# Sorted rows transposed by the DMA queue, and two more buffers for neighbour rows, in a graph kernel with quantile aggregation

## The chip, the cores and the metric

The kernel runs on one core of a Trainium2 chip. A core has five engines that run side by side, each with its own in-order queue of instructions: TensorE (PE; PEld is its loading of weights), VectorE (DVE), ScalarE (ACT), GpSimd (POOL) and SyncE (SP, which here only issues transfers). They meet at semaphores. SBUF holds the working tiles, PSUM what TensorE writes, DRAM the rest. The metric is the device time of one execution in microseconds (us), the median of several runs; less is better.

## The reference

16 graphs of 1024 nodes with 64 channels go through two layers. What is computed:

```python
# layer 0, for each node: drop some neighbours by rank, then quantiles over the rest
nb = (adj_ > 0) & ~eye;  m = nb.sum(-1);  rank = cumsum(nb) - 1
skip = where(m > 10, (m + 1) // 2, 1)
removed = nb & (skip > 1) & mask & ((rank + 1) % skip == 0)
adj_d = where(removed | removed.T, 0, adj_)
agg = 0.25 * q25 + 0.5 * q50 + 0.25 * q75     # of x over the neighbours left, per channel, interpolated
y = relu((x + agg) @ W1 + b1) @ W2 + b2
x = layernorm(x + y * mask)
# layer 1
dh = tanh(concat(x, adj @ x) @ W1' + b1') @ W2' + b2'
x = layernorm(x + dh)
```

The edge update of layer 1 does not reach the output. About 1.6% of the node pairs are edges, so a node has some 10 to 30 neighbours after the dropping. The quantiles need each node's neighbours sorted, channel by channel.

## The kernel before

The graphs are handled in groups of 2, 4, 4, 4 and 2 (`GROUPS`). A group passes through three stages, and stages of different groups run side by side: while one group is in its quantiles, the lists of the next are made and the messages of the one before are finished.

**Lists** (`list_batch`, one graph after the other, in 8 tiles of 128 nodes). SP loads a tile of adjacency `a` (L622, a pool of three buffers that the messages use too) and the tile's rows of `x` into the tail of a row buffer `nb` (L625). DVE makes `nb`, the 0/1 row in bf16 (L623, L626). ACT counts it, TensorE ranks it (L652 to L660), ACT and DVE find the removed neighbours, TensorE and ACT write the kept ones back into `nb` (L672 to L677). Then the nodes of the graph are sorted by their number of neighbours (L685 to L708), and POOL writes each `nb` tile, row by row, to its sorted place in DRAM, in `order` (L712, an indirect DMA, a scatter). An `nb` buffer can be filled anew only after its scatter has read it. `nb` has NT + 1 = 9 buffers for 8 tiles per graph, so tile t of the next graph takes the buffer of tile t-1. `gone`, the removed ones, has 8.

**Quantiles.** After sorting, nodes with like numbers of neighbours lie together, and a group is cut into chunks (`CHUNKS`) that share one number of slots k. For each chunk `fill` puts the neighbours' `x` into slots `slots_a`, and `select` runs a network of min and max on DVE over them (L875), weighs the quantiles on ACT and PE (L897, L899), computes the layer, and scatters the result `y` to DRAM (L916). There are two kinds of fill:

- `Chunk`: DVE extracts the neighbours' numbers from the rows (L825, L827) and POOL gathers `x` by them, one indirect DMA for each slot and tile (L846, 1012 in all).
- `ChunkByPE` (the fourth entry of a `CHUNKS` tuple is 1): TensorE selects rows. For each pair of graphs, which is called a pass here (32 in all), SP loads two blocks of 128 sorted rows x 1024 from `order` into `row_p` (L957, two buffers). TensorE transposes each in 8 blocks of 128 x 128 into PSUM (L960, the single buffer with tag "tr", which the transposes of `nb` at L652 use too), and ACT copies it into `val` (L961), whose two halves are those of the two graphs. TensorE adds up ranks over the nodes and ACT writes them back into `val` (L966 to L970). For each slot k DVE makes a 0/1 matrix `hot` by `val == k` (L982), and TensorE multiplies it with `x`, which was split into three bf16 parts (L990). ACT copies the result into the slots (L1001). `val` has one buffer, so ACT's copy for the next pass waits for the last `hot` of this one; `row_p` waits only for TensorE.

**Messages** (`messages`): layer 1, one graph after the other. `a` is loaded again (L1024), transposed by TensorE (L1029), multiplied with `x` (L1039); DVE adds up `d` (L1049).

The source weaves the stages with `Side.advance`: in each chunk 24 shares are given out, and each stage advances by its part. The order of instructions on an engine is then set by a planner when the program is built, which works from the source's order and from when it expects buffers and inputs to be ready. SP is one in-order queue for all loads but the indirect ones: `a`, `x`, `row`, `row_p`, `degs`, `srt` and slot 0. POOL's queue holds the gathers and both kinds of scatter.

A slow general path behind the fast one (`tc.If(general > 0)`, from L1155 on) is not run with these inputs.

Of the kernel before, what the change touches and what calls it, by code (L numbers as in the profile page):

```python
# [9 lines left out]
F32 = mybir.dt.float32  # L10
F16 = mybir.dt.float16
BF16 = mybir.dt.bfloat16
# [3 lines left out]
ALU = mybir.AluOpType  # L16
# [4 lines left out]
P = 128  # L21
# [6 lines left out]
BINS = 64  # L28
# [388 lines left out]
def kernel(  # L417
# [15 lines left out]
    nc = tc.nc  # L433
    B, N, C = x.shape
    H = w1a.shape[1]
    NT = N // P
# [11 lines left out]
    const = ctx.enter_context(tc.tile_pool(name="const", bufs=1))  # L448


    ident = const.tile([P, P], F32, name="ident")
    make_identity(nc, ident)
    ident_h = const.tile([P, P], BF16, name="ident_h")
    nc.vector.tensor_copy(ident_h, ident)
    off_diag = const.tile([P, P], BF16, name="off_diag")
    nc.vector.tensor_scalar(off_diag, ident, -1.0, 1.0, op0=ALU.mult, op1=ALU.add)
    upper = const.tile([P, P], F32, name="upper")
    nc.gpsimd.memset(upper, 1.0)
    nc.gpsimd.affine_select(out=upper, in_=upper, compare_op=ALU.is_ge, fill=0.0, base=0,
                            pattern=[[1, P]], channel_multiplier=-1)  # L460
    off_diag_f = const.tile([P, P], F32, name="off_diag_f")
    nc.vector.tensor_copy(off_diag_f, off_diag)
    minus_h = const.tile([P, P], BF16, name="minus_h")
    nc.vector.tensor_scalar(minus_h, ident, -1.0, None, op0=ALU.mult)
    far_h = const.tile([P, P], BF16, name="far_h")
# [6 lines left out]
    ones_h = const.tile([P, P], BF16, name="ones_h")  # L472
# [9 lines left out]
    nc.vector.memset(big[:, 1:2], -BIG)  # L482
    eps = const.tile([P, 1], F32, name="eps")
    nc.vector.memset(eps, EPS)
    zero = const.tile([P, BINS], F32, name="zero")
    nc.vector.memset(zero, 0.0)
    number = const.tile([P, B * NT], F32, name="number")
    nc.gpsimd.iota(number, pattern=[[P, B * NT]], base=0, channel_multiplier=1,
                   allow_small_or_imprecise_dtypes=True)
# [92 lines left out]

    sort = ExitStack()
    rows = sort.enter_context(tc.tile_pool(name="rows", bufs=2))
    held = sort.enter_context(tc.tile_pool(name="held", bufs=NT + 1))
    work = sort.enter_context(tc.tile_pool(name="work", bufs=2))
    nets = sort.enter_context(tc.tile_pool(name="nets", bufs=2))
    hbm = sort.enter_context(tc.tile_pool(name="hbm", bufs=1, space=DRAM))
    ps_t = sort.enter_context(tc.tile_pool(name="ps_t", bufs=1, space=PSUM))
# [22 lines left out]
    def list_batch(g, b):  # L612

        nbs, gone = [], []
        for half_b in range(2):
# [3 lines left out]
            for t in range(half_b * HT, (half_b + 1) * HT):  # L619
# [8 lines left out]
                for h in range(2):  # L628
# [15 lines left out]
                                           op0=ALU.is_gt, op1=ALU.mult)  # L644
# [3 lines left out]
            for t in range(half_b * HT, (half_b + 1) * HT):  # L648
                nb, r, col = nbs[t], gone[t], slice(t - half_b * HT, t - half_b * HT + 1)
                p = ps_t.tile([P, N], BF16, name="p_nb", tag="tr")  # L650
# [5 lines left out]
                for h in range(2):  # L656
                    p = ps_m.tile([P, HALF], F32, name="p_rank", tag="rv", bufs=3)
# [9 lines left out]
        for t in range(NT):  # L667
            blk = slice(t * P, (t + 1) * P)
            for h in range(2):
                cols = slice(h * HALF, (h + 1) * HALF)  # L670
                p = ps_m.tile([P, HALF], F32, name="p_val", tag="rv", bufs=3)
# [19 lines left out]
        p = ps_m.tile([P, 512], F32, name="p_tot", tag="m")  # L691
        for t in range(NT):
            nc.tensor.matmul(p[:, :BINS], ones_h, own[:, t], start=t == 0, stop=t == NT - 1)
        base = work.tile([P, BINS + 1], F32, name="base", bufs=1)
        nc.vector.memset(base[:, 0:1], 0.0)
        nc.vector.tensor_tensor_scan(base[:, 1:], zero, p[:, :BINS], 0.0, op0=ALU.add, op1=ALU.add)
        p = ps_m.tile([P, NT, BINS], F32, name="p_at", tag="m")
        nc.tensor.matmul(p, ident, base[:, None, :BINS].to_broadcast([P, NT, BINS]), start=True, stop=False)
        for t in range(NT - 1):
# [222 lines left out]
    class ChunkByPE(Chunk):  # L922
# [13 lines left out]
        def fill(self):  # L936
            g, low = self.g, self.net["low"]
# [4 lines left out]
            at0 = self.t0 * g.run  # L942
            slots = self.net["slots"]
            inside = {at: k for k, at in enumerate(slots)}
            for q in range(g.count // 2):
# [7 lines left out]
                    nc.vector.tensor_scalar(free[:, k - low], degs[:, :, :, 0], float(k), None, op0=ALU.is_le)  # L953
                val = nets.tile([P, NT, 2, P], BF16, name="val", bufs=1)
                for i in range(2):
                    row = nets.tile([P, N], BF16, name="row_p")
                    nc.sync.dma_start(row, g.order[2 * q + i][at0:at0 + P, :N // 2].bitcast(BF16))  # L957
                    p = ps_t.tile([P, NT, P], BF16, name="p_row", tag="tr")
                    for j in range(NT):
                        nc.tensor.transpose(p[:, j], row[:, j * P:(j + 1) * P], ident_h)  # L960
                    nc.scalar.copy(val[:, :, i], p)  # L961

                for c in range(NT - 2, -1, -2):
                    p = ps_m.tile([P, 2, 2 * P], F32, name="p_nth", tag="rv", bufs=3)
# [8 lines left out]
                for s0 in range(0, self.k, 4):  # L973
                    p = ps_m.tile([P, 4, P], F32, name="p_slots", tag="rv", bufs=3)
                    for s in range(s0, min(s0 + 4, self.k), 2):
# [5 lines left out]
                        for e, at in enumerate(duo):  # L981
                            nc.vector.tensor_scalar(hot[:, :, :, e], val, float(inside[at]), None,  # L982
                                                    op0=ALU.is_equal)
# [72 lines left out]
    def prepare(g):  # L1056
        for b in range(g.b0, g.b0 + g.count):
            yield from list_batch(g, b)
        yield from weigh_group(g)
# [37 lines left out]
    for s in range(-LEAD, len(plan)):  # L1097
        j = s + LEAD
# [17 lines left out]
        if s >= 0:  # L1116
            i = plan[s][0]
# [40 lines left out]
    rows = ctx.enter_context(tc.tile_pool(name="rows_g", bufs=2))  # L1158
    held = ctx.enter_context(tc.tile_pool(name="held_g", bufs=NT))
    work = ctx.enter_context(tc.tile_pool(name="work_g", bufs=1))  # L1160
    ones_row = work.tile([P, N], BF16, name="ones_row")
    nc.vector.memset(ones_row, 1.0)  # L1162
    ps_t = ctx.enter_context(tc.tile_pool(name="ps_t_g", bufs=2, space=PSUM))
# [94 lines left out]
    with tc.tile_pool(name="dense", bufs=1) as dense, tc.If(general > 0), tc.For_i(0, B, 1) as b:  # L1258
# [5 lines left out]
        val = dense.tile([P, NT, N], BF16, name="val")  # L1264
        val_t = dense.tile([P, NT, N], BF16, name="val_t")
        for t in range(NT):
            v = neighbours(t, kept, removed, deg[:, t:t + 1])
            nc.vector.tensor_copy(val[:, t], v)
            p = ps_t.tile([P, NT, P], BF16, name="p_val", tag="tr")
# [7 lines left out]
        with tc.For_i(0, C, 1) as c:  # L1277
# [3 lines left out]
            for h in range(2):  # L1281
                p = ps_t.tile([P, HT, P], F32, name="p_row", tag="ta")
# [5 lines left out]
            for k in range(NT):  # L1288
# [3 lines left out]
                if k + 1 < NT:  # L1292
                    nc.vector.tensor_scalar(before[:, k, k + 1:], x_r[:, k + 1:], x_k, None, op0=ALU.is_ge)
                nc.vector.scalar_tensor_tensor(before[:, k, k], x_r[:, k], x_k, upper,
                                               op0=ALU.is_equal, op1=ALU.mult)
                nc.vector.scalar_tensor_tensor(before[:, k, k], x_r[:, k], x_k, before[:, k, k],
                                               op0=ALU.is_gt, op1=ALU.add)
            part = dense.tile([P, NT, 2], F32, name="part")
            for t in range(NT):
                for h in range(2):  # L1300
                    cols = slice(h * HALF, (h + 1) * HALF)
                    js = slice(h * HT, (h + 1) * HT)
                    p = ps_m.tile([P, 512], F32, name="p_cnt", tag="m")
# [5 lines left out]
                    for i, (_, share) in enumerate(TAUS):  # L1309
# [5 lines left out]
                        else:  # L1315
# [3 lines left out]
                                                   op0=ALU.mult, op1=ALU.mult,  # L1319
# [31 lines left out]
```

## Time and profile before

| | us |
|---|---|
| median of 4 runs (3128.2 to 3146.86) | 3137.62 |
| the profiled execution | 3127.18 |
| its span, first to last instruction | 3125.5 |
| PE / DVE / ACT / POOL busy | 2370.9 / 2391.6 / 1575.6 / 1695.1 |
| POOL gathers L846, 1012 of 1336 ns | 1352.3 |
| DVE min and max L875, three largest groups | 356.2, 285.7, 197.5 |
| PE L990 (12288 matmuls) | 694.9 |
| scatter of `nb`, L712, 128 of 1133 ns | 145.0 |
| mean granted TensorE clock | 0.889 of full speed |

In the lines of the profile, "PE p_row L960" is the instruction of line 960 on PE that writes the tile p_row; an arrow `out<-in` names what it writes and reads. In a list of groups, "x512 | 45.3, 226 | 15.9 <-ACT val L961 13.3" is: 512 instructions, busy for 45.3 us together, 226 ns the mean of one; before them the engine stood idle for 15.9 us, of which 13.3 ended when ACT's instruction of L961 was done. In a list of waits, "A <- B: 73.6, 29, 20.4" is: A waited for B, 73.6 us in total, in 29 waits, the longest 20.4. In the slices, the span is cut into 40 equal parts of 78 us, and each digit is the busy share in tenths. In a timeline each row has its start, its length and, in brackets, the engine's idle time before it and what ended it. "SPq" is SP's queue, which issues transfers; what it waits for is the condition of the transfer.

### The profile page before, as it was taken

The page shows a single profiled execution, that of the slowest core. Times are in us where ns is not written, and L with a number is a line of the kernel's source. Part 1 is how long each engine was busy: PE and PEld are TensorE (multiplying, and loading weights), DVE is VectorE, ACT ScalarE, POOL GpSimd, SP SyncE. Part 2 cuts the span into 40 slices and gives each one's busy share as a digit, 9 for nine tenths or more (in the row PEclk, how much of TensorE's full clock was granted, in tenths as well). Part 3 has the DMA queues.
Part 4 walks back from the last instruction along what each step waited for, and adds up shares of the span by engine and source line. Part 5 has one row for each costly group of instructions (what it writes and reads, how often), then busy time and mean ns, then how long its engine had stood idle before and what let it go on. Part 6 is the DMA issues. An engine that isn't in the chain of part 4 may idle for free. (4 is left out here: it accounts for less than half of the span.)

```text
span 3125.5 us, 65767 instructions
## 1 busy us (share of the span) xinstructions
PE 2370.9 (76%) x24920; PEld 1885.5 (60%) x25076; DVE 2391.6 (77%) x5580; ACT 1575.6 (50%) x4045; POOL 1695.1 (54%) x1512
## 2 busy tenths in 40 slices
PE   4456875769686997859888997787799376677977
PEld 2244663457574776647767775576677365466755
DVE  3359984679799889969999888888999397666741
ACT  5624656746354556544566566334464244243543
POOL 3165774356587376766663866485456555343300
PEclk9778998889898998989999998898899698888988
DMA  2520433333323333243334243123232231122222
GB/s 94 163 58 21 117 111 99 103 89 100 90 67 84 103 100 83 47 121 106 89 94 125 64 129 96 40 62 118 69 82 65 64 84 43 54 73 53 80 64 79
DMA packets 221333, 264.34 MB, mean 85 GB/s; under 512 B 147443, under 2 KB 148050, under 8 KB 221008
## 3 DMA queue, kind: packets, MB, share of 16 engines
q1 hardware_dynamic: 174288, 189.31, 20.8%
q0 software_dynamic: 46720, 70.74, 8.7%
q8 instruction: 199, 3.26, 0.4%
q14 instruction: 126, 1.03, 0.1%
HBM read 218.20 MB, written 46.40 MB: 85 GB/s over the span
## 5 line engine op out<-in xcount | busy, mean ns | idle before, releaser
L846 POOL DMA_INDIRECT slots_a<-in_x_dram,idx x1012 | 1352.3, 1336 | 724.7 <-issue 265.5
L990 PE MATMUL p_slots<-hot,parts 128*64 128x256 bf16 (+1 forms) x12288 | 694.9, 269 | 135.2 <-DVE hot L982 130.2
L990 PEld LDWEIGHTS <-parts 128*64 128x64 bf16 x12288 | 631.6, 113 | 174.0 <-issue 99.1
L875 DVE TENSOR_TENSOR slots_b<-slots_a 128x256 f32<-128x256 f32 (+14 forms) x582 | 356.2, 627 | 96.8 <-DMA slots_a<-in_x_dram,idx 64.7
L916 POOL DMA_INDIRECT x<-y,ids x128 | 174.0, 1359 | 361.0 <-DVE y L558 214.7
L982 DVE TENSOR_SCALAR hot<-val 128x2048 bf16<-128x2048 bf16 x456 | 308.4, 694 | 20.1 <-PE p_slots L990 16.6
L899 PE MATMUL p_g<-ident,terms 128*64 128x128 f32 x1988 | 279.2, 293 | 57.5 <-ACT terms L897 56.9
L899 PEld LDWEIGHTS p_g<-ident,terms 128*64 128x64 f32 x1988 | 238.3, 148 | 90.4 <-ACT terms L897 72.6
L875 DVE TENSOR_TENSOR slots_a<-slots_b 128x256 f32<-128x256 f32 (+11 forms) x526 | 285.7, 555 | 0.6
L1039 PE MATMUL p_msg<-adj_t,x_n 128*64 128x128 f32 x2048 | 277.2, 289 | 7.9 <-ACT adj_t L1030 4.2
L1039 PEld LDWEIGHTS p_msg<-adj_t,x_n 128*64 128x64 f32 x2048 | 237.3, 145 | 31.8 <-issue 10.6
L630 ACT ACTIVATE gone<-nb 128x512 bf16<-128x512 bf16 x256 | 159.9, 628 | 157.6 <-DVE nb L626 156.0
L1001 ACT COPY slots_a<-p_slots 128x512 f32<-128x512 f32 (+2 forms) x136 | 73.0, 537 | 300.2 <-PE p_slots L990 246.1
L1029 PE MATMUL p_adj<-ident,a 128*128 128x128 f32 x1024 | 185.8, 295 | 43.5 <-ACT adj_t L1030 22.1
L660 PE MATMUL p_rank<-reach,nb_t 128*128 128x128 bf16 (+3 forms) x956 | 172.7, 312 | 58.9 <-ACT nb_t L654 50.7
L662 ACT ACTIVATE gone<-p_rank,s 128x512 bf16<-128x512 f32 x256 | 166.2, 684 | 97.1 <-PE p_rank L660 82.1
L825 DVE MAX8 key<-code 128x8 f16<-128x1024 f16 x170 | 207.2, 1219 | 1.7
L875 DVE TENSOR_TENSOR slots_b<-slots_b 128x256 f32<-128x256 f32 (+11 forms) x310 | 197.5, 637 | 0.4
L712 POOL DMA_INDIRECT order<-nb,at_i x128 | 145.0, 1133 | 94.8 <-issue 40.6
L660 PEld LDWEIGHTS <-nb_t 128*128 128x128 bf16 x1024 | 95.2, 103 | 164.5 <-ACT nb_t L654 78.1
L1049 DVE TENSOR_TENSOR d<-p_d,b2b_r 128x64 f32<-128x64 f32 x128 | 28.1, 219 | 209.3 <-PE p_d L1048 206.7
L1030 ACT COPY adj_t<-p_adj 128x512 f32<-128x512 f32 x256 | 149.4, 583 | 75.4 <-PE p_adj L1029 73.3
(189 smaller groups left out, 4573.7 us busy)
## 6 DMA issues: line engine op xcount, KB each, us to landing
a<-in_adj_dram SPq DMA_DIRECT2D x256, 512.0 KB
row_p<-order SPq DMA_DIRECT2D x64, 256.0 KB
slots_a<-in_x_dram,idx POOLq DMA_INDIRECT x1012
row<-order SPq DMA_DIRECT2D x192, 64.0 KB
nb<-in_x_dram SPq DMA_DIRECT2D x128, 32.0 KB
row<-order SPq DMA_DIRECT2D x32, 128.0 KB
x_s<-in_x_dram SPq DMA_DIRECT2D x16, 256.0 KB
x_n<-x SPq DMA_DIRECT2D x16, 256.0 KB
```

Of the source, the lines that this page charges most:

```text
L630: nc.scalar.activation(r[:, cols], nb[:, cols], AF.Copy, accum_out=m[:, h, t - half_b * HT:t - half_b * HT + 1])
L660: nc.tensor.matmul(p[:, c * P:], nb_t[:, (h * HT + c) * P:(h * HT + c + 1) * P], reach[:, :HALF - c * P], start=False, stop=c == HT - 1)
L662: nc.scalar.activation(r[:, h * HALF:(h + 1) * HALF], p, AF.Abs, bias=biases[h][:, col], scale=2.0)
L825: nc.vector.max(key[:, t, r:r + 8], code)
L846: nc.gpsimd.indirect_dma_start(out=self.a[:, at[k], t, :], out_offset=None, in_=x_rows, in_offset=bass.IndirectOffsetOnAxis(ap=idx[:, t, k ...
L875: nc.vector.tensor_tensor(view(rb, ra, [(d[0], d[1 + side]) for d in dims]), view(ab, aa, [(d[0], d[1]) for d in dims]), view(bb, ba, [(d[ ...
L899: nc.tensor.matmul(p[:C, col], terms[:, i], ident, start=False, stop=t == e - 1 and first + i == places - 1)
L916: nc.gpsimd.indirect_dma_start(out=g.x1, out_offset=bass.IndirectOffsetOnAxis(ap=g.local[:, self.t0 + t:self.t0 + t + 1], axis=0), in_=y[: ...
L982: nc.vector.tensor_scalar(hot[:, :, :, e], val, float(inside[at]), None, op0=ALU.is_equal)
L990: nc.tensor.matmul(p[i * C:(i + 1) * C, o:o + w], g.parts[2 * q + i][:, c, h], hot[:, c, i, :w], start=c == 0 and h == 0, stop=c == NT - 1 ...
L1029: nc.tensor.transpose(p[:, j, :], a[:, col:col + P], ident)
L1039: nc.tensor.matmul(p[C:2 * C, :QUART], x1[:, j, :], adj_t[:, j, :], start=(j == 0), stop=(j == NT - 1))
```

## The change

Three edits:

1. The two blocks of sorted rows of a pass in `ChunkByPE.fill` are transposed by the transfer itself: a DMA transpose, issued on SP, reads 128 rows x 1024 bf16 from `order` and writes 128 partitions x 8 x 128 straight into one half of `val`. The tile `row_p`, TensorE's 16 transposes and ACT's two copies of a pass are gone.
2. `held`, the pool of the `nb` tiles, has NT + 3 = 11 buffers and no longer 9.
3. Two constants leave the memory of the fast path. `off_diag` in bf16 is made only for the general path, and `off_diag_f` comes straight from `ident`. `zero` is gone: the running sum in `list_batch` multiplies by ones where it added zeros. With `row_p` (4096 bytes in each partition), `zero` and `off_diag` (256 each) they make up most of the 4640 bytes that two more `nb` tiles take.

```diff
-    off_diag = const.tile([P, P], BF16, name="off_diag")
-    nc.vector.tensor_scalar(off_diag, ident, -1.0, 1.0, op0=ALU.mult, op1=ALU.add)
...
-    nc.vector.tensor_copy(off_diag_f, off_diag)
+    nc.vector.tensor_scalar(off_diag_f, ident, -1.0, 1.0, op0=ALU.mult, op1=ALU.add)
...
-    zero = const.tile([P, BINS], F32, name="zero")
-    nc.vector.memset(zero, 0.0)
...
-    held = sort.enter_context(tc.tile_pool(name="held", bufs=NT + 1))
+    held = sort.enter_context(tc.tile_pool(name="held", bufs=NT + 3))
...
-        nc.vector.tensor_tensor_scan(base[:, 1:], zero, p[:, :BINS], 0.0, op0=ALU.add, op1=ALU.add)
+        nc.vector.tensor_tensor_scan(base[:, 1:], ones_h[:, :BINS], p[:, :BINS], 0.0, op0=ALU.mult, op1=ALU.add)
...
                 val = nets.tile([P, NT, 2, P], BF16, name="val", bufs=1)
                 for i in range(2):
-                    row = nets.tile([P, N], BF16, name="row_p")
-                    nc.sync.dma_start(row, g.order[2 * q + i][at0:at0 + P, :N // 2].bitcast(BF16))
-                    p = ps_t.tile([P, NT, P], BF16, name="p_row", tag="tr")
-                    for j in range(NT):
-                        nc.tensor.transpose(p[:, j], row[:, j * P:(j + 1) * P], ident_h)
-                    nc.scalar.copy(val[:, :, i], p)
+                    nc.sync.dma_start_transpose(
+                        val[:, :, i], g.order[2 * q + i][at0:at0 + P, :N // 2].bitcast(BF16))
...
+    off_diag = work.tile([P, P], BF16, name="off_diag")
+    nc.vector.tensor_copy(off_diag, off_diag_f)
     ones_row = work.tile([P, N], BF16, name="ones_row")
```

## The prediction

> **What bounds the kernel now.** I read the page's shares and slices first, then the list of waits, then the waits of SP's queue, then the timeline where a long wait lies, and last the tiles that the change touches.
>
> ```profile
> PE 2370.9 (76%) x24920; PEld 1885.5 (60%) x25076; DVE 2391.6 (77%) x5580; ACT 1575.6 (50%) x4045; POOL 1695.1 (54%) x1512
> ...
> PE   4456875769686997859888997787799376677977
> ...
> DVE  3359984679799889969999888888999397666741
> ```
>
> No engine is the bound by itself. DVE is nearly full from slice 9 to slice 31, PE close behind, and the idle time (734 us on DVE) lies at the start, at the end and in lumps between. So a saving counts where it closes a lump, and only in part where it makes one of two full engines shorter.
>
> ```profile
> DVE nb L626 <- DMA order<-nb,at_i: 73.6, 29, 20.4
> ...
> SPq L625 <- DMA order<-nb,at_i: 369.0, 80, 67.0
> ...
> SPq L957 <- PE p_row L960: 209.6, 29, 53.7
> ```
>
> The first two lines are the buffers: DVE stood 73.6 us in 29 waits, and SP's queue 369 us, until a scatter had read an old `nb`. The last is the queue waiting for a `row_p` buffer. The largest lump, by the timeline from 803 to 830 us:
>
> ```profile
> 819.73 1.00 POOL L846 DMA_INDIRECT slots_a<-in_x_dram,idx  x1 [0.30 <-DMA slots_a<-in_x_dram,idx]
> 821.03 1.00 POOL L846 DMA_INDIRECT slots_a<-in_x_dram,idx  x1 [0.30 <-issue]
> 823.67 0.98 POOL L712 DMA_INDIRECT order<-nb,at_i  x1 [0.17 <-issue]
> 824.96 0.96 POOL L712 DMA_INDIRECT order<-nb,at_i  x1 [0.30 <-issue]
> 826.22 1.12 POOL L712 DMA_INDIRECT order<-nb,at_i  x1 [0.30 <-issue]
> 826.53 0.69 DVE L626 TENSOR_SCALAR nb<-a 128x1024 bf16<-128x1024 f32 x1 [20.45 <-DMA order<-nb,at_i]
> 827.26 0.63 ACT L630 ACTIVATE gone<-nb 128x512 bf16<-128x512 bf16 x1 [21.89 <-DVE nb L626]
> ```
>
> The scatter stands behind a row of gathers of 1.3 us each on POOL; DVE waits 20.45 us for the first one, about 2.9 us after its issue, and ACT behind it. The transposes that the change removes:
>
> ```profile
> L960 PE MATMUL p_row<-ident_h,row_p 128*128 128x128 bf16 x512 | 45.3, 226 | 15.9 <-ACT val L961 13.3 <-DMA row_p<-order 2.1 <-ACT nb_t L654 0.4
> L961 ACT COPY val<-p_row 128x1024 bf16<-128x1024 bf16 x64 | 64.7, 1012 | 28.3 <-DVE hot L982 11.3 <-PE p_row L960 10.4 <-DVE low L687 6.3
> ```
>
> Pipelined, 512 transposes are 45.3 us of busy PE, not 512 x 226 ns; ACT's copies are 64.7 us. Their loads come early: SP issued them up to 196 us before the first copy that uses them.
>
> **What the Trainium skill says.** "DMA: Bandwidth & Descriptors", section on the anatomy of one DMA: a DMA has about 2.0 us of fixed time, and a wait for a semaphore happens on the issuing sequencer, before dispatch. The trace agrees: the SP queue stands still in L625 and L957 while nothing behind them leaves. The same page, "Rules for kernel authors", has the DMA transpose issued from SP or ACT only, so the change can't leave that in-order queue for GpSimd's; no run here shows a transpose yet. The two prices below are from that page (latency section: 261 GB/s with a non-contiguous middle dimension) and from "VectorE: DVE Perf Modes", the three transpose paths (1309 ns for 128x128 bf16 by DMA, 390 ns by TensorE; the trace has 219 ns as TensorE's median, so the page's figures are not this kernel's).
>
> **The change, part by part.** The profiled execution is 3127.2 us, 3125.5 of it span; its time is 10 us under the median of 3137.6. I make the sum on its trace and move the median by it.
>
> *Buffers of `nb`, 9 to 11.* Tile t of the next batch takes the buffer of tile t-3 and no longer of t-1, so tiles 1 and 2 also run ahead of the scatter, and tile 3 meets the wait that tile 1 met. The wait does not go; two of seven tiles move to the front of it. The order on each engine is not the source's: the trace shows loads of `row_p` leaving ahead of the `degs` load that stands before them. So I do not assume that tile 3 comes later on DVE than tile 1 did: by the timeline tiles 1 to 3 of the batch in the fence ran at 827, 830 and 842 us, in haste, as soon as the buffers were free. In the opening stretches (before 200 us, and 500 to 600), where little else runs, the batch is a chain: tiles 1 to 7 of the second batch start at 78 to 93 us, 2.3 us each with what hangs on them. Two tiles at four such boundaries: 4 x 2 x 2.3 = 18 us off. From 600 to 2400 us the waits of L626 add up to 46.5 us; I take a third, 15 us, since SP is also freed earlier for the adjacency loads behind L625. Bounds: 0 (all waits move on to tile 3) and -73.6.
>
> *PE and ACT.* Out go 45.3 us of PE and 64.7 us of ACT, with 26.5 us in which PE waited for those copies (13.3 before L960 and 13.2 before L966). ACT is half idle, so its part counts nothing by itself. Of PE's 72 us I take a fifth, 15: PE was busier than 95% in only two of the 31 windows of 100 us. Bounds: 0 and -72.
>
> *DMA transposes.* 64 loads of 256 KB become 64 transposes of the same bytes, 2 in each of 32 passes. The destination is `val`, one buffer, so SP must now wait until the last `hot` of the pass before has read it (L982). Before, only ACT's copy waited for that, and the loads lay ready. Behind the waiting transpose stand, on SP, adjacency loads (three buffers, used by lists and messages), rows, `degs`, slot 0 and the sorted numbers; DVE (L623) and PE (L1029, L960's successors at L966) wait for them. For each of passes 2 to 32 I took from the timeline the end of the last `hot`, the next issue on SP after it (mean 5.5 us later, a total of 170), and the first rank matmul (L966), 5 to 76 us after it and mostly about 20. With d the delay of SP, X the time of one transfer and 0.5 us for the second issue, the lateness is d + 0.5 + 2X + 2.0 less that gap, where positive. The table sums it over passes:
>
> | X, us | late in total, us | passes late |
> |---|---|---|
> | 1 | 26 | 2 |
> | 3 | 37 | 5 |
> | 5 | 62 | 8 |
> | 8 | 129 | 18 |
> | 10.5 | 231 | 24 |
>
> X is between 1.0 us (256 KB at 261 GB/s) and 10.5 us (8 x 1309 ns, if nothing of eight blocks overlaps). I take 1.0, as an estimate from the page's rate: a price for one small block is mostly latency. 25 of its 26 us are one place, at 2669 us, where SP stood 25 us before a load of `x_n`. A lower bound is -10: passes in which the copy had come at once may start sooner, since 16 transposes and two copies, some 5 us, are gone.
>
> *Constants.* `off_diag`, `zero` and the scan's other operand are set-up or one instruction of 0.29 us per batch; nothing.
>
> Sum: -18 - 15 - 15 + 26 = **-22 us**, 3105 for the profiled execution, **3115** on the median, 0.7% less.
>
> **The rivals.** *The queue decides (slower).* Place: SP before each pass's rank matmuls; price: X. From X of about 4 us on, the lateness eats the 48 us gained. At 8 us it is +81, so 3219; at 10.5 us +183, so 3320. For it: SP holds nothing else back so often as a late reader, `val` has one buffer, the lead of the loads is lost, and a held queue also delays adjacency loads that the sum leaves out. Against it: in most passes some 20 us lie between `hot` and the rank matmuls, filled with other work.
>
> *The buffers carry it (a larger gain).* If tile 3 comes so late on DVE that four fifths of the 73.6 us go, -59, and PE's 45.3 us count in full: 3127 - 59 - 45 + 26 = 3049, so about 3059. For it: at 2101 us DVE stood 12.4 us with the next two tiles 19 and 26 us away. Against: tiles crowd up behind every scatter.
>
> *Nothing shows.* The waits move to tile 3 (0), PE's relief lies beside DVE's work (0), a third of the 26 us is felt: +9 us, 3146. It does what it says in each case: the transposed rows are the same values in the same places.
>
> **How the numbers follow.** Forecast 37%, the queue 36%, nothing shows 15%, buffers 10%, and 2% for a loss by another order of the instructions alone. A measurement of this kernel can tell about 0.5% (16 us) from no change: the runs shown spread over 19 us. Of the forecast's 37%, a tenth lies within that. So faster 0.44, same 0.18, slower 0.38. The forecast's own range is 3085 to 3135. The whole range, 3040 to 3270, takes in nearly all of the buffers' case and the queue's up to X of some 9 us, and leaves out 4% below and 14% above.
>
> **What would show it.** Right, if the page has no L960 and L961, PE down by about 45 us and ACT by 65, DVE's wait at L626 between 40 and 60 us and now first at a batch's fourth tile, SP's wait at the transposes for `hot`, and first rank matmuls that wait for the transposes' landing 30 us or less in all. Wrong, if PE waits at L966 or DVE at `hot` for `val` by 100 us or more, if one transpose holds the SP queue or the DMA engines for over 4 us, or if the adjacency loads (L623, L1029), 48.7 us of DVE's waits now, double. If L626's wait falls below 20 us, the buffers were worth more than I gave them.

## The result, and the profile after

The changed kernel takes 3151.91 us (median of 34 runs) against 3139.6 us (55 runs) for the kernel before. The measured ratio is 1.0056 with a 95% interval from 1.0041 to 1.0071: 0.56%, some 17.6 us, slower. (It is not the ratio of the two medians, which are 12.3 us apart.) The profiled executions are 3153.92 and 3127.18 us, 26.7 us apart, so the two traces show about 9 us more than the ratio does. Two more traces of before's order of instructions (h1 and h2 below) have spans of 3110.9 and 3137.2 us where the first has 3125.5, so 26 us between two single traces is within what kernels of one speed do; what is read from a pair of traces has to be larger than it is among these three. In three of the five sessions below every kernel took some 21% longer (the one before 3801 to 3813 us), so a ratio is only read inside its session, and it leaves out executions over 1.5% above the fastest of the same kernel, in those three sessions up to two thirds of them.

The busy row of the page of the changed kernel:

```profile
PE 2358.9 (75%) x24407; PEld 1864.8 (59%) x24564; DVE 2392.0 (76%) x5579; ACT 1516.5 (48%) x3979; POOL 1713.5 (54%) x1512
```

ACT fell by 59.1 us, most of the 64.7 that its copies took. PE fell by only 12.0 us, although 512 transposes of 45.3 us are gone. So its other matmuls, as many as before, took 33 us longer, at a mean granted clock of 0.878 for 0.889 in these two traces. The slot matmuls, before and after:

```profile
L990 PE MATMUL p_slots<-hot,parts 128*64 128x256 bf16 (+1 forms) x12288 | 694.9, 269 | 135.2 <-DVE hot L982 130.2
...
L982 PE MATMUL p_slots<-hot,parts 128*64 128x256 bf16 (+1 forms) x12288 | 708.3, 270 | 122.6 <-DVE hot L974 116.9
```

DVE's work did not change; its idle time grew by 26.3 us, nearly the whole growth of the span. The largest of its waits that bear on the lists, and the one at `d`, after the change:

```profile
DVE d L1041 <- PE p_d L1040: 230.7, 62, 31.1
...
DVE nb L622 <- DMA order<-nb,at_i: 75.4, 18, 19.0
...
DVE a L619 <- DMA a<-in_adj_dram: 68.9, 34, 5.6
```

(L622, L619 and L1041 are L626, L623 and L1049 of before.) The wait that the two buffers aimed at is what it was, 73.6 before, in 18 portions for 29. By tile of the batch, added up from the trace, 56.7 of the 73.6 us lay at the second tile before; after, 70.3 of the 75.4 lie at the fourth, and next to nothing at the three ahead of it. The wait for the adjacency loads rose to 68.9; before it was

```profile
DVE a L623 <- DMA a<-in_adj_dram: 48.7, 27, 5.5
```

Together 122.3 became 144.3: 22 us, of the size of the loss. The wait at `d` rose by as much, from 206.7 to 230.7, and other waits fell by about 20. But `d` stands at 219.2 in a kernel that is as fast as before (h2) and at 198.8 in e1, the slowest kernel of the last table below; it doesn't follow the loss, and nothing is built on it.

The SP queue of the changed kernel:

```profile
SPq L1016 <- PE p_adj L1021: 509.7, 72, 21.7
SPq L621 <- DMA order<-nb,at_i: 344.9, 68, 66.8
SPq L952 <- DVE hot L974: 207.6, 17, 26.0
SPq L618 <- DVE nb L622: 153.3, 39, 33.5
SPq L618 <- PE p_adj L1021: 133.0, 21, 23.4
```

L952 are the transposes, waiting for the last `hot`, about as long as the loads had waited for `row_p` (209.6). Longer than before are the waits of L618, the lists' load of `a`; before, at L622, they were

```profile
SPq L622 <- DVE nb L626: 111.3, 30, 16.9
...
SPq L622 <- PE p_adj L1029: 76.1, 18, 13.1
```

The transposes themselves, by the view of their tile and by the view of who waits for their line:

```profile
L952 SPq DMA_TRANSPOSE val<-order x64: 1232/1294/3757, 98.0 to 2921.6; - x64
```

```profile
who waited for it (us, times):
  PE p_nth L958: 11.0, 6
```

One issue holds SP for 1.29 us in the median (a load of `row_p` held it for 0.34), but PE waited for the landing 11.0 us in all, in 6 waits.

When was the time lost? At 775 us the changed kernel was 17.8 us ahead (the first rank matmul of the seventh pass against the same one before). Half of this was gone at the next pass (9.1 us ahead at 862); from there to 1513 us it fell to 12.4 us behind, and at the end to 26.7. Not all such steps come from the change: h2 falls back by 11 us between 1353 and 1444 us with the order of before. Two waits of DVE in this stretch, in the timeline of the changed kernel, each at a batch's fourth tile:

```profile
1015.15 0.69 DVE L622 TENSOR_SCALAR nb<-a 128x1024 bf16<-128x1024 f32 x1 [10.39 <-DMA order<-nb,at_i]
```

```profile
1169.55 0.69 DVE L622 TENSOR_SCALAR nb<-a 128x1024 bf16<-128x1024 f32 x1 [17.53 <-DMA order<-nb,at_i]
```

In the kernel before, the same two batches met their scatter with almost no wait:

```profile
1006.24 0.69 DVE L626 TENSOR_SCALAR nb<-a 128x1024 bf16<-128x1024 f32 x1 [0.30 <-DMA order<-nb,at_i]
```

```profile
1156.83 0.69 DVE L626 TENSOR_SCALAR nb<-a 128x1024 bf16<-128x1024 f32 x1 [0.83 <-DMA order<-nb,at_i]
```

The first of these scatters left POOL at 1012.30 us for 1003.10. POOL's timeline ahead of it, in the kernel before:

```profile
930.94 2.91 POOL L916 DMA_INDIRECT x<-y,ids  x1 [1.48 <-DMA x<-y,ids]
935.30 1.00 POOL L916 DMA_INDIRECT x<-y,ids  x1 [1.45 <-DMA x<-y,ids]
937.20 2.32 POOL L846 DMA_INDIRECT slots_a<-in_x_dram,idx  x1 [0.90 <-ACT node_t L1041]
939.83 1.07 POOL L846 DMA_INDIRECT slots_a<-in_x_dram,idx  x1 [0.30 <-issue]
```

and in the changed one:

```profile
929.55 0.96 POOL L912 DMA_INDIRECT x<-y,ids  x1 [1.57 <-DMA x<-y,ids]
941.33 1.93 POOL L912 DMA_INDIRECT x<-y,ids  x1 [10.82 <-DVE off L826]
943.56 1.05 POOL L842 DMA_INDIRECT slots_a<-in_x_dram,idx  x1 [0.30 <-DVE slots_b L871]
...
954.06 11.49 POOL L842 DMA_INDIRECT slots_a<-in_x_dram,idx  x1 [0.30 <-issue]
```

After 935 us the kernel before goes on with gathers. The changed one has a scatter of `y` (L912) in their place, which must wait for DVE, and the gathers and the scatters of `nb` stand behind it. The order of POOL's queue is another one. What the place costs can be measured between the same two instructions, from the 271st gather to this scatter of `nb`, with 39 gathers and 9 scatters of `y` from the first of these to the second in either kernel: 81.7 us before (81.8 in h1, 84.7 in h2), 99.2 in the changed one. Two things lie in these 17.5 us more that aren't there before: the wait of 10.82 us at the scatter of `y`, and a single gather, the last row above, that held POOL for 11.49 us. This gather, the 281st, takes 10.3 or 11.5 us in every trace of the changed kernel and of e1, and no gather of the stretch takes over 3 us in the three traces of before's order. Why it takes so long isn't known. The second place adds nothing: from the 307th gather to the scatter that it waits for the changed kernel takes 161.7 us and the one before 160.2; that scatter is late because POOL came late to the stretch.

How far the order differs, one can count in the trace: for each scatter of `y`, the gathers that started before it (the scatters numbered from 0). In the changed kernel 28 of the 128 counts differ. The places at which such a scatter was moved ahead in one of the kernels and then waited over 5 us (gathers ahead of it, and POOL's wait at it in us; both runs of before and h2 agree in every one of the 128 counts; e3, whose own loads hold it up, is left out):

```
scatter of y    before, h1, h2   changed      transposes, 9   transposes, 10   e4
no. 8           134, 0.3         126, 11.4    126, 10.7       129, 0.3         128, 0.3
no. 15          175, 0.3         177, 0.3     173, 14.6       173, 15.6        180, 0.3
no. 21          291, 0.3         271, 10.8    271, 24.6       271, 15.4        289, 0.3
no. 28          318, 0.3         306, 32.6    306, 48.9       306, 39.4        306, 33.2
no. 45          434, 0.3         434, 0.3     421, 18.9       424, 0.3         421, 21.2
no. 53          539, 0.3         539, 0.3     520, 0.3        539, 0.3         519, 24.4
no. 60          567, 0.3         569, 0.3     554, 46.1       554, 44.0        554, 38.7
sum over 5 us   -                54.8         163.8           114.4            117.5
```

Not all of such a sum is new: at no. 28 the kernel before stood 44.5 us too, before a gather that came at about the same time (1061 us). In the changed kernel, that leaves 22.2 of the 54.8.

### The profile page after: what moved, and what is told of

Its sections match the earlier page's. It is cut to its first block, busy times and chain, and to the rows that moved or that the text cites. A ratio compares the mean times of both kernels' runs of the same rounds, so it can differ in the third digit from the quotient of the medians.

```text
span 3152.2 us, 64647 instructions
## 1 busy us (share of the span) xinstructions
PE 2358.9 (75%) x24407; PEld 1864.8 (59%) x24564; DVE 2392.0 (76%) x5579; ACT 1516.5 (48%) x3979; POOL 1713.5 (54%) x1512
## 5 line engine op out<-in xcount | busy, mean ns | idle before, releaser
L842 POOL DMA_INDIRECT slots_a<-in_x_dram,idx x1012 | 1382.3, 1366 | 724.5 <-issue 276.6
L982 PE MATMUL p_slots<-hot,parts 128*64 128x256 bf16 (+1 forms) x12288 | 708.3, 270 | 122.6 <-DVE hot L974 116.9
L982 PEld LDWEIGHTS <-parts 128*64 128x64 bf16 x12288 | 639.0, 114 | 164.3 <-issue 127.0
L912 POOL DMA_INDIRECT x<-y,ids x128 | 162.1, 1266 | 408.5 <-DVE y L554 232.6
L626 ACT ACTIVATE gone<-nb 128x512 bf16<-128x512 bf16 x256 | 159.4, 627 | 156.6 <-DVE nb L622 155.3
L656 PE MATMUL p_rank<-reach,nb_t 128*128 128x384 bf16 (+3 forms) x958 | 176.0, 313 | 41.8 <-ACT nb_t L650 35.0
L1041 DVE TENSOR_TENSOR d<-p_d,b2b_r 128x64 f32<-128x64 f32 x128 | 28.0, 219 | 231.4 <-PE p_d L1040 230.7
```

Of the source, the lines that this page charges most:

```text
L626: nc.scalar.activation(r[:, cols], nb[:, cols], AF.Copy, accum_out=m[:, h, t - half_b * HT:t - half_b * HT + 1])
L656: nc.tensor.matmul(p[:, c * P:], nb_t[:, (h * HT + c) * P:(h * HT + c + 1) * P], reach[:, :HALF - c * P], start=False, stop=c == HT - 1)
L842: nc.gpsimd.indirect_dma_start(out=self.a[:, at[k], t, :], out_offset=None, in_=x_rows, in_offset=bass.IndirectOffsetOnAxis(ap=idx[:, t, k ...
L912: nc.gpsimd.indirect_dma_start(out=g.x1, out_offset=bass.IndirectOffsetOnAxis(ap=g.local[:, self.t0 + t:self.t0 + t + 1], axis=0), in_=y[: ...
L982: nc.tensor.matmul(p[i * C:(i + 1) * C, o:o + w], g.parts[2 * q + i][:, c, h], hot[:, c, i, :w], start=c == 0 and h == 0, stop=c == NT - 1 ...
```

## The experiments

The first theory after the result: the transposes cost (SP's queue held for `val`, issue time), and the buffers give some of it back. The rival: the buffers cost. A third, called C in the expectations, came with the first four runs: no part carries a time by itself, the time follows the moments at which DVE meets the scatters behind POOL's gathers. D there is SP's wait for `hot`, E the issue time of a transpose.

### First session (before: 3139.2 us)

**e1_transpose_only**: the changed kernel with 9 buffers.

```diff
-    held = sort.enter_context(tc.tile_pool(name="held", bufs=NT + 3))
+    held = sort.enter_context(tc.tile_pool(name="held", bufs=NT + 1))
```

> The DMA transposes and the constants, with 9 nb buffers as before. Theory A (the two buffers cost the time: DVE's wait for the scatter moved from a batch's second tile to its fourth, where it falls on fuller stretches): this kernel stands at 0.993 to 1.000 of before, DVE's wait at L622 is again mostly at the second tile. Theory B (the transposes cost it: 1.3 us of SP for each issue and the wait for hot make the adjacency loads late, DVE's wait at L619 was 48.7 us and is 68.9): 1.004 to 1.010 of before, and L619 stays near 69 us. Theory C (the time is that of another order of the instructions, and no part carries it): anything from 0.995 to 1.008.

Measured: 1.0187 (1.0146 to 1.0227), 3197.46 us, beyond the ranges of all three theories. Its waits:

```profile
POOL x L912 <- DVE y L554: 309.3, 11, 55.9
...
DVE nb L622 <- DMA order<-nb,at_i: 142.1, 27, 22.3
...
DVE a L619 <- DMA a<-in_adj_dram: 64.4, 40, 10.0
```

DVE's wait for scatters nearly doubled, by 68.5 us, and the span grew by 69.3. Of the 142.1 us, 133.2 lie at the second tile, as before. Yet at 775 us this kernel was 17.6 us ahead, as much as the changed one: the gain of the opening came with the transposes and needs no buffer. POOL waited 309.3 us for `y`, where the kernel before had 214.7. The stretch that took 81.7 us before and 99.2 in the changed kernel took 108.4 here, 24.6 of them at the scatter of `y`.

**e2_transpose_10_buffers**: the same with `NT + 2`.

> The DMA transposes with 10 nb buffers, one less than the changed kernel. Theory A: between the kernel with 9 and the changed one, the wait now at a batch's third tile. Theory B: as the changed kernel, 1.004 to 1.010. Theory C: off the line between 9 and 11 buffers by over 0.3%.

Measured: 1.0095 (1.0058 to 1.0132), 3162.79 us. DVE's wait for scatters is 70.2 us, for `a` 74.6. One buffer takes back half of what the transposes cost, two take back 70% (1.0056, from another set of runs).

**e3_buffers_only**: 11 buffers, transposes by TensorE. Memory doesn't hold both the buffers and `row_p`, so its loads share the two buffers of `row`:

```diff
-                    row = nets.tile([P, N], BF16, name="row_p")
+                    row = nets.tile([P, N], BF16, name="row", tag="row")
```

> 11 nb buffers, rows transposed by TensorE as before; to find the memory, row_p takes its turns in the two buffers of row. Theory A: 1.004 to 1.010 of before, the wait at the fourth tile 65 to 75 us. Theory B: 0.993 to 1.000. Theory C: anything from 0.995 to 1.008.

Measured: 1.0305 (1.0268 to 1.0343), 3227.65 us, again beyond all three ranges. This says little of the buffers: the loads now stand in SP's queue behind readers of `row` (149.5 us for `code`, 208.4 for `free`), and PE waited 81.2 us for `a`.

**e4_buffers_rows_in_hot**: the same, with the two rows in one of the buffers of `hot`.

```diff
+                pair = nets.tile([P, NT, 2, 2, P], BF16, name="hot").rearrange("p a b c d -> p (a b c d)")
...
-                    row = nets.tile([P, N], BF16, name="row_p")
+                    row = pair[:, i * N:(i + 1) * N]
```

> 11 nb buffers, TensorE's transposes, and the sorted rows of a pass loaded into one of the two hot buffers, so that the load waits for a late reader, as the DMA transpose does, but costs SP only 0.34 us. Theory A: as the buffers alone. Theory B, if it is the wait and not the issue time: slower than the buffers alone by 0.5% or more; if it is the issue time: as the buffers alone. Theory C: apart from the buffers alone by up to 0.5% either way.

Measured: 1.0104 (1.0064 to 1.0145), 3167.28 us. DVE's wait for scatters is 57.9 us, the least of the four so far, and its wait for `a` 97.8, the most. The waits of SP's queue:

```profile
SPq L621 <- DMA order<-nb,at_i: 369.2, 74, 65.0
SPq L618 <- DVE nb L622: 180.6, 41, 26.2
SPq L618 <- PE p_adj L1026: 143.3, 19, 28.7
SPq L954 <- DVE hot L979: 94.6, 9, 33.5
```

SP stands at L618 until one of the three buffers of `a` is free. These two waits of L618 add up to 187.4 us in the kernel before and 188.9 in e1 (9 buffers each), 224.5 in e2 (10), 286.3 in the changed kernel and 323.9 here (11 each). So, for SP, the buffers of `nb` shift the limit to the next pool, that of `a`, which the messages use too. That holds with transposes of either kind. DVE's wait for `a` doesn't follow from it alone: in e1 it is 64.4 us for 48.7, though SP stands at L618 no longer than before. And e4 isn't a clean run of the buffers: the rows wait for `hot` here (94.6 us), and PE waits 45.4 us for their landing.

### Three sessions (before: 3800.87, 3803.26 and 3812.99 us)

Four kernels on the transposes' own price. **e5_two_val** is e1 with a second `val` (`bufs=2`), so that SP needn't wait for the last `hot`. **e6_staged** is e1 with the transposes into a tile of their own, which ACT copies:

```diff
+                    row = nets.tile([P, NT, P], BF16, name="row_t")
                     nc.sync.dma_start_transpose(
-                        val[:, :, i], g.order[2 * q + i][at0:at0 + P, :N // 2].bitcast(BF16))
+                        row, g.order[2 * q + i][at0:at0 + P, :N // 2].bitcast(BF16))
+                    nc.scalar.copy(val[:, :, i], row)
```

**e7_from_act** is the changed kernel with the transposes issued on ACT (`nc.scalar.dma_start_transpose`). **e8_one_more_buffer** is the kernel before with 10 buffers of `nb`, the third edit, and one `row_p`.

> DMA transposes, 9 nb buffers, two val buffers, so that SP need not wait for the last hot; the 1.3 us of issue stay. The same with one val stood at 1.019 of before. Theory D (SP's wait for hot costs it: what stands behind comes late): 0.995 to 1.004. Theory E (the issue time or the small packets cost it): 1.012 to 1.020. Theory C (another order of the instructions, no part by itself): between them or beyond, and the lateness shows up in DVE's wait for the scatters (L622), 142 us with one val and 74 before, and not at the transposes.

> DMA transposes into two staging tiles in the place of row_p, and ACT copies each into val as before: the loads keep their lead, ACT's copies and their wait for hot stand where they stood, only TensorE's transposes are gone. 9 nb buffers. Theory D: 0.992 to 1.003. Theory E: 1.010 to 1.020. Theory C: as in the run with two val, off from it by over 0.4%.

> The changed kernel with its transposes issued from ACT's queue, so that SP neither waits for hot nor gives 1.3 us for each; ACT does, where its copy waited before. Theory D and theory E: 0.990 to 1.002 of before, 0.4% or more under the changed kernel; DVE's wait for adjacency (L619, 68.9 us) back near 49. Theory C: no nearer than 0.3% to either.

> TensorE's transposes, 10 nb buffers, one row_p buffer (for the memory). With the DMA transposes the tenth buffer took 0.9% off. If buffers help whatever the transposes: 0.990 to 0.998. If they only mend what the transposes spoil: 1.000 to 1.005. Theory C: anything from 0.995 to 1.015.

The four were then run once more, in another session:

> Again the DMA transposes with 9 nb buffers and two val buffers; before, it ran on a chip on which all kernels took 21% longer, with PE idle for what the profile does not show, and stood at 1.001 there. On a chip like that of the first runs: theory D (SP's wait for hot costs it) 0.995 to 1.004; theory E (issue time, small packets) 1.012 to 1.020; theory C (another order of the instructions) 1.005 to 1.012 or beyond, with DVE's wait for the nb scatters well over 74 us.

> Again the changed kernel with its transposes issued from ACT. Theories D and E: 0.990 to 1.002 of before, DVE's wait for adjacency near 49 us. Theory C: over 1.003, or with a wait at the scatters that differs from the changed kernel's 75 us by 30 us or more.

> Again the transposes into staging tiles with ACT's copies kept, 9 nb buffers. Theory D: 0.992 to 1.003. Theory E: 1.010 to 1.020. Theory C: apart from the run with two val by over 0.4%.

> Again TensorE's transposes with 10 nb buffers and one row_p buffer. If buffers help whatever the transposes: 0.990 to 0.998. If they only mend what the transposes spoil: 1.000 to 1.005. Theory C: anything from 0.995 to 1.015.

and in a third one, two of them beside the two kernels of the first session:

> The changed kernel itself, beside its variants on one chip. It stood at 1.0056 of before. On a chip like the first it should stand there again; on one where all runs take 3800 us, theory D (SP's wait for hot) gives 1.003 to 1.010, theory C (order of the instructions alone) anything from 0.990 to 1.010.

> DMA transposes with 9 nb buffers and one val. 1.0187 in the first call. Theory D: 1.010 to 1.020 wherever it runs, and over the kernel with two val by 1% or more. Theory C: its distance to the others changes with the chip by over 0.7%.

> DMA transposes, 9 nb buffers, two val buffers. Theory D: 1% or more under the same kernel with one val, 0.99 to 1.002 of before. Theory E (issue time): level with the one val within 0.4%. Theory C: under it on one chip and not on another.

> The changed kernel with transposes issued from ACT. Theories D and E: 0.4% or more under the changed kernel in this call, 0.990 to 1.001 of before. Theory C: level with it within 0.3%, or above.

| ratio, by before's time | 3800.87 us | 3803.26 us | 3812.99 us |
|---|---|---|---|
| two `val` | 1.0012 (0.9985 to 1.0039) | 0.9907 (0.9878 to 0.9935) | 0.9904 (0.9861 to 0.9947) |
| staged, ACT copies | 1.0057 (1.0025 to 1.0088) | 1.0017 (0.9983 to 1.0051) | |
| issued on ACT, 11 buffers | 0.9999 (0.9968 to 1.0029) | 0.9935 (0.9905 to 0.9965) | 0.989 (0.9847 to 0.9933) |
| TensorE, 10 buffers, one `row_p` | 1.002 (0.9993 to 1.0047) | 0.9994 (0.9969 to 1.0019) | |
| the changed kernel | | | 0.9857 (0.9819 to 0.9896) |
| transposes, 9 buffers | | | 0.9822 (0.977 to 0.9874) |

The last two rows need care. The 0.9822 rests on two executions of six; the median of all six is at 0.997. The changed kernel's 0.9857 rests on all of its six. Two `val`, by the medians of all its executions, stand at 0.9974, 0.9955 and 0.9955, so most of the 1% by which its ratio moves is made by the executions left out.

Three things follow. The sign is another one here: the changed kernel, which cost 0.56%, gains 1.4%, and e1's kernel, which cost 1.9%, doesn't lose. A second `val` and issue on ACT aren't faster than what they were to mend. But these sessions can't settle D and E: the loss isn't there, and where it is, neither of the two remedies was run. Against D stands only that SP waits for `hot` in e1 no longer (209.7 us) than for `row_p` before (209.6); against E, that PE waited for the landing of the transposes 11.0 us in the changed kernel, 13.2 in e1 and 17.5 in e2. And ratios that differ by 1% or less from one session to another mean nothing. The waits of the changed kernel in the third of these sessions:

```profile
PE p_slots L982 <- issue: 294.3, 289, 34.7
...
DVE hot L974 <- remote: 209.5, 17, 50.8
...
DVE nb L622 <- DMA order<-nb,at_i: 30.6, 15, 5.7
```

PE stood 294.3 us for "issue" before the slot matmuls, where the first trace of this kernel names `hot` (116.9 us) and 1.0 us of issue; DVE stood 209.5 us at `hot` for a releaser that the view can't place, and the wait for scatters fell to 30.6 us. The mean granted clock of this trace is 0.815, where the first one has 0.878. POOL's order is that of the first trace, count by count, and its `y` scatters wait as before (17.7 us at no. 21, 43.4 at no. 28), but DVE waits for scatters less than half as long. That fits the idea of C, that the moved order costs only where DVE meets it, but the kernel before was not traced in these sessions, and C's own range for this run (0.990 to 1.010) missed too. Why the change gains 1.4% there wasn't settled: that PE, which is then the slower engine, has fewer instructions would explain e1's kernel, but the staged one has them away too and gains nothing.

### Last session (before: 3132.15 us)

**h1_before_again** is the kernel before itself; **h2_constants_only** is it with the third edit alone.

> The kernel before itself, measured against itself, to see what a ratio of these runs is worth and what its waits look like beside the others on this chip. If the intervals are honest, its ratio is 1.000 with both ends within 0.004. If the ratio is off by 0.5% or more, the ratios within 1% of each other in this study tell nothing by themselves. DVE's wait for the scatters (L626) some 70 us, as in the profile before.

> The kernel before with the third edit alone: the constants and the scan's second operand, the same number of instructions in every batch. If the time follows only the work, nothing: 0.998 to 1.002, within 6 us. If another set-up alone shifts the moments at which DVE meets the scatters, the ratio is outside 0.996 to 1.004 and DVE's wait at the scatters differs from that of the kernel before by over 15 us.

Measured: 0.9988 (0.996 to 1.0016) and 0.9998 (0.997 to 1.0027). A kernel against itself is off by 0.1% here, so the 0.56% of the changed kernel and the 0.9% to 1.9% of e1, e2 and e4 are taken as differences. The constants cost nothing that these runs can tell. The waits of h1 and of h2:

```profile
DVE nb L626 <- DMA order<-nb,at_i: 66.1, 31, 16.3
...
DVE a L623 <- DMA a<-in_adj_dram: 47.2, 28, 5.8
```

```profile
DVE nb L622 <- DMA order<-nb,at_i: 75.7, 30, 19.1
...
DVE a L619 <- DMA a<-in_adj_dram: 43.9, 29, 5.7
```

These two waits add up to 113.3 and 119.6 us; with 122.3 of the first trace that is a spread of 9 us for kernels of one speed. h2 has every scatter of `y` at the same count of gathers as before, and on DVE the `nb` tiles of all batches at the same places among the slots and `hot` instructions. So it is no test of another order: the edit didn't make one.

### What the runs say together

| kernel | ratio | us over before | DVE for `nb` + `a` | POOL idle ahead of scatters of `y` |
|---|---|---|---|---|
| before | 1 | | 73.6 + 48.7 = 122.3 | 361.0 |
| h1, before again | 0.9988 | -4 | 66.1 + 47.2 = 113.3 | 345.9 |
| h2, constants | 0.9998 | -1 | 75.7 + 43.9 = 119.6 | 355.4 |
| changed | 1.0056 | 18 | 75.4 + 68.9 = 144.3 | 408.5 |
| e2, transposes, 10 | 1.0095 | 30 | 70.2 + 74.6 = 144.8 | 482.9 |
| e4, 11, TensorE | 1.0104 | 33 | 57.9 + 97.8 = 155.7 | 473.4 |
| e1, transposes, 9 | 1.0187 | 59 | 142.1 + 64.4 = 206.5 | 516.0 |

(Ratio less one, times the median of before in the session.) e3 stays out, since its own loads hold it up. The three kernels of before's order are alike in all columns; in the other four the two waits of DVE are longer where the loss is larger, 22, 22, 33 and 84 us over before (the first two don't tell 18 us from 30), and so, nearly in the same order, is what POOL stood for `y`. The last column can be read off one row of the groups each, of before and of e1:

```profile
L916 POOL DMA_INDIRECT x<-y,ids x128 | 174.0, 1359 | 361.0 <-DVE y L558 214.7 <-DMA x<-y,ids 79.5 <-DVE idx L831 31.9
```

```profile
L912 POOL DMA_INDIRECT x<-y,ids x128 | 174.4, 1362 | 516.0 <-DVE y L554 309.3 <-DMA x<-y,ids 81.0 <-DVE off L826 53.3
```

POOL's work is the same 174 us; it stood 155 us longer ahead of it (and 74 us less ahead of gathers, 651.0 for 724.7). The account that fits is this: a scatter of `y` that is put ahead of gathers makes POOL wait for DVE, the gathers and the next `nb` scatters come later, and DVE waits for those. What is shown: the order was changed, in each kernel in the same way in every session, waits stand where it was changed, and at one place, ahead of the scatter at 1012 us, POOL took 17.5 us longer, by it and by a slow gather. Not shown is that the old order would give the time back: a kernel with the transposes and POOL's order of before wasn't run.

One rival is as large as the loss and stays open: TensorE's granted clock, the share of full speed that the records show. It is 0.880 in the mean over the changed kernel's executions, and 0.886 over 52 of the kernel before, in the first session and the last. Among these 52 it runs from 0.879 to 0.891, and the time falls by some 3.5 us for each 0.001 more. By that slope alone, an estimate, the lower clock would go with some 21 us in the changed kernel, where the loss is 18; with 47 in e1 (0.873), where it is 59; with 40 in e2 (0.875), where it is 30; and with 25 in e4 (0.879), where it is 33. So it puts e2 and e4 the wrong way round and is short of e1's loss, but it is large enough to be the most of each. In the slower sessions a lower clock comes without a loss (two `val` in the first of them: 0.809 for before's 0.816, at a ratio of 1.0012), which speaks against it. Whether the lower clock costs the time in the fast sessions, or comes with the waits, no run here tells.

## Why the prediction was wrong

The whole range, 3040 to 3270, held the time; the forecast's own, 3085 to 3135, did not, and the direction was wrong: -22 us were forecast and +18 came. The step that failed, as far as the runs part the edits, is the price of the transposes. Without the buffers' -33 the prediction's terms leave -15 + 26 = +11 for them; e1, transposes with 9 buffers, measured +59. The two buffers then took 41 us off (from e1 to the changed kernel, in two sets of runs), near the 33 forecast, but DVE's wait for scatters is what they shortened (142.1 to 75.4), to what it was before the change. In e4, not a clean run, 11 buffers without DMA transposes stand at +33, so the parts don't simply add up. By its steps:

- **"The wait does not go; two of seven tiles move to the front of it"**: right, to the tile. What failed is the line after it, which took a third of L626's 46.5 us off all the same, "since SP is also freed earlier for the adjacency loads behind L625". Over the whole change the wait stayed (75.4 for 73.6), and the adjacency loads came later, not earlier: DVE's wait for them rose by 20.2 us. Together that is +22 where -15 stood. Of the 20.2 us, 15.7 are there in e1 already, so it isn't the buffers alone that made them late, though SP did meet the three buffers of `a` with the changed kernel's 11 (286.3 us at L618 for 187.4).
- **The opening, -18 by the buffers**: such a gain was there, 17.8 us at 775 us, but e1 had it with 9 buffers (17.6). That the size came out was luck: it came with the transposes, how was not traced, and it was gone by 1285 us.
- **PE and ACT, -15**: PE's 45.3 us became 12.0, since the matmuls that stayed took 33 us longer at the lower clock of that trace. The prediction has no term for the clock.
- **DMA transposes, +26 by lateness**: as a landing price too high, 11.0 us of PE's waits. The price that counted wasn't in the table: with the transposes' 59 us in e1 goes a wait of DVE for scatters that is 68.5 us longer, while SP's wait for `hot`, 209.7, is no more than the 209.6 that the loads had waited before.
- **"2% for a loss by another order of the instructions alone"**: this is, as far as the traces show, why the price came out so wrong, and it is argued, not shown. The prediction had written that "the order on each engine is not the source's", and then laid every part on the order of before. POOL's queue was read for one place, as it stood, and not asked what might be put in front of what. The place, a scatter of `y` ahead of gathers, is on an in-order queue, of the kind that it had looked at on SP alone.
- **The queue decides (the slower rival)** gave the right sign by the wrong step. "DMA: Bandwidth & Descriptors" of the Trainium skill (latency section), from which X was estimated, was the better of the two prices. In the 28 passes whose packets can be told apart, the last packet of the first transpose ended 2.9 us after its issue and that of the second 4.8 us after the first's issue, in the median. With the 0.5 and 2.0 us of the prediction's sum that makes X an estimated 1.2 us. (The 2.0 us stand in the page's section on a transfer issued by GpSimd; these were issued by SP.) This rival was to decide from X = 4 us on.

Of the signs it named, ACT's 59 us, the gone lines, the fourth tile and the 30 us for landing came true. PE's 45 and the wait at L626 "between 40 and 60 us" did not. Two small slips bear on none of this: the `row_p` loads led their copies by up to 248 us, not 196, and the shares add up to 0.43, 0.19 and 0.38 for the 0.44, 0.18 and 0.38 given.

## What to carry to other kernels

Where a planner sets the order, a change on some engines can change the order on others: here POOL, whose instructions the change doesn't touch, got another order in every kernel with DMA transposes or another number of buffers. After such a change, compare first, queue by queue, which instruction that waits has come ahead of which that don't, on POOL's queue as on SP's. Count buffers along the whole way of a tile: with two more in one pool SP stood longer at the next pool, which was also shared with another stage. Run the kernel against itself and its parts in one session, and compare the granted clocks, before a difference under 1% is explained.

## What the hardware showed beside this

A DMA transpose of 256 KB took 1.29 us of SP for its issue where the plain load took 0.34, and the packets of the whole kernel rose from 221333 to 279696. The order of a queue is the same in every session, but speed isn't: one chip gave 3800.9 us for the kernel before in one session and 3132.2 in a later one. In the slower sessions POOL's gathers were the faster ones (1170 ns against 1366 for the same kernel), while PE stood for "issue" and the granted clock of the kernel before was 0.814 to 0.816 in the mean, for 0.886 in the others.
